# Query and key stacks of two cross attentions moved from tile to tile instead of by DRAM, and token scales spread by TensorE, in a two-layer decoder

## The chip, the cores and the metric

The kernel runs on one core of one Trainium2 chip. The metric is the time of one execution on the device in microseconds (us), the median of several runs. Lower is better. The trace is of one further execution, taken by the hardware profiler.

## What is computed

The input x is 8 batches of 256 tokens with 512 channels, a context of the same size goes with it, and everything is float32. Two decoder layers follow each other. Every block adds to x and normalises (post-norm):

```python
x = _layernorm(x + _L0_attn_ref(x, ...))            # power attention, 16 heads of 128
x = _layernorm(x + _L0_xattn_ref(x, ctx, ctx))      # 16 heads of 32, causal softmax
x = _layernorm(x + _L0_ffn_ref(x, ...))             # router, 8 bases, shared expert
x = _layernorm(x + _L1_attn_ref(x, ...))            # multi-query, plus a memory
x = _layernorm(x + _L1_xattn_ref(x, ctx, mask, ...))# 16 heads of 32, int8-like projections
x = _layernorm(x + _L1_ffn_ref(x, ...))             # 8 experts of 16, top 2
```

The change concerns the two cross attentions. The first uses x itself as queries and the context as keys and values, without projections:

```python
scores = einsum('bhqd,bhkd->bhqk', q, kj) * SCALE   # causal; then softmax, times values
```

The second quantises x by token (a scale `sx` for each token), projects it with quantised weights, and so needs each token's scale as a factor along the token axis of the projected queries:

```python
s = maximum(max(abs(x), axis=-1) / 127, EPS); qx = clip(round(x / s), -127, 127)
q = einsum('bnc,oc->bno', qx, qw) * (sx * sw) + bq
```

## The kernel before

Tokens are worked on in four groups g of two batches (512 tokens), and channels in four chunks kc of 128, which are four heads of 32. Six stages follow each other, overlapping at their ends: the first attention until about 760 us of the trace, the first cross attention until 1078, the first feed-forward until 1650, the second attention until 2045, and then the second cross attention with the last feed-forward.

**Stacks.** float32 products are made of two parts each, a high part rounded to fp32r and the rest as a low part, as high*high + low*high + high*low. In the cross attentions a head has 32 channels, so the three products fit on top of each other in one contraction of 96 rows: the queries are stacked as (high, low, high), `QO = (0, 1, 0)`, and the keys as (high, high, low), `KO = (0, 0, 1)`. A stack is a tile of 96 partitions by 4 heads by 512 tokens. The parts are made with 128 channels on 128 partitions (4 heads of 32). To become a stack, head j's 32 partitions must move to partitions 32i to 32i+31 of part i. Before, that goes by DRAM: `stack_out` (line 1101) writes the high and the low part, 256 KB each, to a buffer of the ring `rs` (four buffers), and `stack_in` (line 1107) reads three transfers of 256 KB, one for each part i, into the stack.

**First cross attention** (`l0_xattn`). For each of 16 chunks (g, kc), `stacks` turns x (TensorE), makes the high part xh on ScalarE (L1218) and the low part xl on VectorE (L1222), and sends both out. Both tiles have one buffer (`bufs=1`). `keys` sends out the context's parts cth and ctl, and `stacked` reads both stacks into `qs[kc % 2]` and `ks[kc % 2]`: tiles b_q and b_k for even chunks, two tiles named b_pair for odd ones. The first two chunks are made earlier, during the first attention, by `first_stacks`, through their own DRAM buffers bq and bk. `attend` then makes, for two batches and four heads, scores (TensorE, L1331), maxima (VectorE, L1345), exponentials (ScalarE, L1352), transposes (L1365), and sums with the values (L1381). Beside it run `later_keys` and `later_values`: keys and values of the second cross attention, kept in DRAM (ke, ve) until they are read there.

**Second cross attention** (`l1_xattn`). `Quantising` finds each token's scale on VectorE (L1549 to L1551), rounds on GpSimd, and turns the result by TensorE through the PSUM bank m2 (one buffer). `scales_out` sends the 512 scales (tile xts) to a DRAM buffer dsx (L2223, single words) and reads them back into all 128 partitions as tile sxb (L2225). `queries_keys` projects (L2243), multiplies by both scales on VectorE (tq, L2247), makes th (ScalarE, L2251) and tl (VectorE, L2255), one buffer each, and sends both out. `load` has `stacked` read the query stack back and the key stack from ke, and `values` read v (L2278). `attend` makes scores (L2291), maxima with the mask (L2306), exponentials (L2315), transposes (L2329) and sums (L2348). In the last group (g = 3) the two batches are worked on one after the other and each reads its half of the stack.

**What sets the order.** All DMAs of these stages are issued by SyncE (SP), in order: one that waits holds all behind it. The order on every engine is made before the kernel runs. Each step of the work is entered with a planned time (`plan.at`). `listed` then plays the whole program: at each point it takes, among the steps that may go within a window (`W_A` to `W_D`, `WINDOW`) and a slack (`SLACK`) of the earliest start, the one with the earliest planned time, moved by an amount for its kind from the table `MOVED`. Durations come from `occupied`, with the latencies `LP`, `LA` and `LV`. Every engine is then held to the order found. So a change of these constants can move any instruction of the program.

Of the kernel before, what the change touches and what calls it, by code (L numbers as in the profile page):

```python
# [13 lines left out]
F32 = mybir.dt.float32  # L14
# [7 lines left out]
P = 128  # L22
# [17 lines left out]
SB, W_A, W_B, W_C, WC, WDD = -3000, 26.2, 23.9, 17.8, -5, -30  # L40
LP, LA, LV = 0.325, 0.235, 0.215
SE, WINDOW, SLACK, QL_D, ML_D, W_D, QX_D, TP = -350.0, 35.5, 0.033, 20, 14, 22.8, 0, 10
# [6 lines left out]
def occupied(i, mode):  # L49
# [44 lines left out]
    ("Ctx", "load_tokens"): -4.45,  # L94
    ("Loading", "high"): 4.8,
    ("Loading", "load"): 8.85,
    ("Loading", "low"): -3.6,
    ("Norming", "apply"): 8.25,
    ("Norming", "minus"): -2,
    ("Norming", "scale"): 7.15,  # L100
    ("Norming", "stats"): 3.5,
    ("Pool", "close"): -4.25,
    ("Pool", "open"): 1.05,
    ("Prepared", "high"): 2.35,
    ("Prepared", "load"): 1.7,
    ("Prepared", "low"): 6.15,
    ("Prepared", "scale"): 2.7,
    ("Prepared", "scales"): 0.85,
    ("Prepared", "store"): 0.5,
    ("QKV", "open"): 5.05,  # L110
    ("Quantising", "out"): -8.85,
    ("Quantising", "scale"): 1.9,
    ("Quantising", "turn"): -2.95,
    ("Quantising", "whole"): -5.4,
    ("Transposing", "high"): -4.2,
    ("Transposing", "low"): -7.3,
    ("Transposing", "turn"): -11.85,
    ("l0_attn", "add"): -0.15,
    ("l0_attn", "constants"): 4.05,
    ("l0_attn", "decay"): 7.05,  # L120
    ("l0_attn", "decay_broadcast"): 4,
    ("l0_attn", "high"): 2.45,
    ("l0_attn", "load"): 2.25,
    ("l0_attn", "log_sigmoid"): 6.65,
    ("l0_attn", "low"): -4.9,
    ("l0_attn", "mul"): -12,
    ("l0_attn", "norms_turn"): -10.3,
    ("l0_attn", "out"): -2.05,
    ("l0_attn", "proj"): 5.15,
    ("l0_attn", "scores"): 2.7,  # L130
    ("l0_attn", "split"): 11.15,
    ("l0_attn", "split_gate"): -1.4,
    ("l0_attn", "square"): -4.4,
    ("l0_attn", "sums"): 4.5,
    ("l0_attn", "sums_out"): 4.4,
    ("l0_attn", "turn"): -3.55,
    ("l0_ffn", "act"): -5.65,
    ("l0_ffn", "add"): 1.4,
    ("l0_ffn", "choose"): -3.2,
    ("l0_ffn", "counts"): 2.9,  # L140
    ("l0_ffn", "down"): -0.5,
    ("l0_ffn", "load"): 3.6,
    ("l0_ffn", "logits"): -0.3,
    ("l0_ffn", "logits_out"): -8.55,
    ("l0_ffn", "mixtures"): 3.95,
    ("l0_ffn", "mul"): -12,
    ("l0_ffn", "proj"): -3.75,
    ("l0_ffn", "split"): 1.55,
    ("l0_ffn", "turn"): 0.9,
    ("l0_ffn", "turn_back"): 3.35,  # L150
    ("l0_xattn", "add"): 3.9,
    ("l0_xattn", "bias"): 0.45,
    ("l0_xattn", "constants"): -5.8,
    ("l0_xattn", "high"): -0.95,
    ("l0_xattn", "keys"): 9.4,
    ("l0_xattn", "load"): -11.6,
    ("l0_xattn", "load_bias"): -1.25,
    ("l0_xattn", "load_context"): 2.75,
    ("l0_xattn", "low"): 0.7,
    ("l0_xattn", "maxima"): -2.4,  # L160
    ("l0_xattn", "more_constants"): 2.6,
    ("l0_xattn", "out"): 1.75,
    ("l0_xattn", "probs"): 6.05,
    ("l0_xattn", "proj"): 4.8,
    ("l0_xattn", "scale"): -5.8,
    ("l0_xattn", "stacked"): -8.7,
    ("l0_xattn", "sums"): 1.9,
    ("l0_xattn", "sums_out"): 8.6,
    ("l0_xattn", "turn"): 6.25,
    ("l0_xattn", "turn_back"): 7.3,  # L170
    ("l0_xattn", "values"): 10.95,
    ("l1_attn", "add"): 4.8,
    ("l1_attn", "elu_exp"): 5.65,
    ("l1_attn", "elu_relu"): 2.65,
    ("l1_attn", "elu_split"): -2.75,
    ("l1_attn", "high"): -7.6,
    ("l1_attn", "keys_high"): 1.55,
    ("l1_attn", "keys_in"): -0.5,
    ("l1_attn", "keys_values_tiles"): -12,
    ("l1_attn", "low"): -12,  # L180
    ("l1_attn", "memories"): 2.35,
    ("l1_attn", "memory_add"): -1.4,
    ("l1_attn", "memory_out"): 5.6,
    ("l1_attn", "memory_scale"): -1.15,
    ("l1_attn", "out"): -8.75,
    ("l1_attn", "probs"): 2,
    ("l1_attn", "proj"): -1.55,
    ("l1_attn", "queries_in"): -4.7,
    ("l1_attn", "reduce"): 8.3,
    ("l1_attn", "scale"): 12,  # L190
    ("l1_attn", "scores"): 3.2,
    ("l1_attn", "split"): 8.3,
    ("l1_attn", "sums"): 12,
    ("l1_attn", "sums_out"): -7.7,
    ("l1_attn", "turn"): 4.95,
    ("l1_attn", "values_copy"): 4.15,
    ("l1_attn", "values_out"): -0.55,
    ("l1_attn", "weights"): 11,
    ("l1_ffn", "act"): -12,
    ("l1_ffn", "act_add"): 1.6,  # L200
    ("l1_ffn", "act_tanh"): -5.55,
    ("l1_ffn", "add"): -0.35,
    ("l1_ffn", "choose"): -6.45,
    ("l1_ffn", "chosen"): 3.1,
    ("l1_ffn", "gate"): -0.95,
    ("l1_ffn", "gated"): 0.6,
    ("l1_ffn", "proj"): -2.4,
    ("l1_ffn", "split_low"): 0.8,
    ("l1_ffn", "turn"): -0.9,
    ("l1_ffn", "up"): 0.5,  # L210
    ("l1_ffn", "weights"): -9.55,
    ("l1_ffn", "write"): -5.45,
    ("l1_xattn", "add"): -0.6,
    ("l1_xattn", "bias_x"): -1.4,
    ("l1_xattn", "high"): -4.7,
    ("l1_xattn", "low"): -5.85,
    ("l1_xattn", "masks_in"): 1.7,
    ("l1_xattn", "maxima"): 0.3,
    ("l1_xattn", "out"): 2.15,
    ("l1_xattn", "probs"): 0.7,  # L220
    ("l1_xattn", "proj"): -0.2,
    ("l1_xattn", "put"): -2.5,
    ("l1_xattn", "scale"): -5.3,
    ("l1_xattn", "scales_out"): 8.55,
    ("l1_xattn", "scores"): 2.2,
    ("l1_xattn", "stacked"): -1.7,
    ("l1_xattn", "sums"): 6.05,
    ("l1_xattn", "sums_out"): -7.85,
    ("l1_xattn", "sums_turned"): 8.4,
    ("l1_xattn", "turn"): 1.75,  # L230
    ("l1_xattn", "turn_back"): 3.8,
    ("l1_xattn", "values"): -6.6,
# [877 lines left out]

def halves_in(K, dst, d, order):

    for i in range(2):
        for part, s in enumerate(order):
            ins = K.nc.sync.dma_start(
                f32(dst[64 * i + 16 * part : 64 * i + 16 * part + 16]),
                d[s].rearrange("(p i d) t -> i d p t", i=2, d=16)[i],
            )
    return ins
# [34 lines left out]
def l0_xattn(K, plan, before, late_from, pair, wk, bk, wv, bv):  # L1154
# [49 lines left out]
    def stacks(plan, t0, src, kc, pool, tag, scale, ring, out):  # L1204
# [15 lines left out]
        def low():  # L1220
            l = pool.tile([P, 512], FR, tag=tag + "l", name=tag + "l", bufs=1)
            nc.vector.scalar_tensor_tensor(l, whole(), scale, f32(st["h"]), ALU.mult, ALU.subtract)  # L1222
            stack_out(K, out(), st["h"], l)
# [5 lines left out]

    def stack(u, n):  # L1230
        u[n] = K.dram.tile([2, P, 512], F32, tag="rs", name="rs", bufs=4)
        return u[n]

    def first_stacks(us):
# [11 lines left out]
        for kc in range(2):  # L1246
            us[kc]["qd"], us[kc]["kd"] = (K.scratch(f"b{n}{kc}", [2, P, 512]) for n in "qk")
            t = U_A * (20 + 2 * kc)
            stacks(before, t, lambda: c["t"], kc, pre, "k", 1.0, None, lambda kc=kc: us[kc]["kd"])
            stacks(before, t + U_A, lambda: K.x[0], kc, pre, "q", SCALE, "v", lambda kc=kc: us[kc]["qd"])  # L1250

    def queries_keys(t0, g, kc, c, u):


        def keys():
            stack_out(K, stack(u, "kd"), c["t"].h[:, kc, :], c["t"].l[:, kc, :])
# [1465 lines left out]
```

## Time and profile before

| | |
|---|---|
| median of 3 runs | 2397.88 us (2394.03 to 2402.05) |
| profiled execution, its own time | 2399.13 us |
| its span in the trace | 2397.4 us |
| granted TensorE clock, mean | 0.958 |
| TensorE, VectorE, ScalarE, GpSimd busy | 91%, 63%, 46%, 30% |
| moved by DMA | 226.83 MB, 36.0% of 16 engines' span |

Busy time in the stages (us):

| stretch | PE | DVE | ACT | DMA share |
|---|---|---|---|---|
| 0 to 760 | 731.56 | 461.16 | 325.06 | 0.20 |
| 760 to 850 | 66.54 | 59.93 | 49.00 | 0.60 |
| 850 to 1078 | 205.11 | 130.57 | 137.53 | 0.71 |
| 1078 to 1650 | 548.40 | 292.91 | 116.49 | 0.27 |
| 1650 to 2045 | 358.57 | 291.25 | 207.53 | 0.43 |
| 2045 to 2110 | 54.31 | 47.64 | 49.88 | 0.73 |
| 2110 to 2397 | 227.01 | 222.81 | 208.55 | 0.46 |

In the trace PE is TensorE's matmuls, PEld its weight loads, DVE is VectorE, ACT ScalarE, POOL GpSimd, SPq the queue of SyncE. L1107 is line 1107 of the kernel. `b_pair<-rs` is an operation that writes tile b_pair and reads rs. The chain is the work that ended last, followed back from the end. "A <- B: 13.9, 17, 3.6" says that A waited for B for 13.9 us in all, 17 times, at most 3.6.

### The profile page before, as it was taken

To read this page: it belongs to the slowest core of one execution; us is meant where nothing else is said; L and a number is where in the kernel's file an instruction comes from. 1 tells how busy PE (TensorE), PEld (TensorE's weight loads), DVE (VectorE), ACT (ScalarE), POOL (GpSimd) and SP (SyncE) were. 2 spreads that over 40 slices of the span, in tenths; PEclk is the share of its full clock that TensorE was granted. 3 is DMA by queue.
4 is the path that set the end of the run, shared out by engine and by line. 5 is a ranking of instruction groups with operands and counts; after the bars stand their busy time and mean duration, and the time that the engine had idled before them with its cause. 6 is when DMAs were issued, how large, how long until landed. Compare 5 with 4: busy or idle time off the path is not lost.

```text
span 2397.4 us, 36873 instructions
## 1 busy us (share of the span) xinstructions
PE 2191.5 (91%) x12779; PEld 1670.0 (70%) x12800; DVE 1506.3 (63%) x3563; ACT 1094.0 (46%) x2697; POOL 718.0 (30%) x978
## 2 busy tenths in 40 slices
PE   7999999899999689988989999998999997878885
PEld 5888877688887567666778778886556564546663
DVE  5655666656556655555655554444777876778885
ACT  3443444444444565654211321112456554678884
POOL 3544444544444211111112201001112323523233
PEclk9999999999999899998999999999799998899997
DMA  4111122112112777752563201103454353765630
GB/s 141 49 40 45 58 76 71 45 57 80 40 36 84 201 215 206 205 167 80 56 147 119 69 33 53 36 1 98 84 93 87 79 92 78 172 157 141 177 80 36
DMA packets 146266, 226.83 MB, mean 95 GB/s; under 512 B 23680, under 2 KB 46848, under 8 KB 145824
## 3 DMA queue, kind: packets, MB, share of 16 engines
q1 hardware_dynamic: 146080, 224.48, 36.0%
q8 instruction: 102, 1.67, 0.3%
q14 instruction: 84, 0.69, 0.1%
HBM read 162.43 MB, written 57.79 MB: 92 GB/s over the span
## 4 chain that ended last, share of the span: by engine, by line
PE 65%; DVE 14%; DMA 7%; ACT 7%; issue 4%; POOL 2%; SPq 1%; ACTq 0%; DVEq 0%; POOLq 0%
PE v L665 5%; PE v L667 5%; PE v L666 5%; PE w L667 3%; PE w L665 3%; PE w L666 3%; PE mm L652 3%; PE mm L665 3%; PE mm L667 3%; PE mm L666 3%; PE z L665 2%; PE z L667 2%; PE z L666 2%; PE w L652 2%; PE z L652 2%
## 5 line engine op out<-in xcount | busy, mean ns | idle before, releaser
L1038 POOL TENSOR_TENSOR x<-x,ot 128x512 f32<-128x512 f32 x128 | 171.7, 1341 | 261.3 <-ACT ot L1037 199.8
L2029 DVE TENSOR_REDUCE nm<-w 128x2 f32<-128x512 f32 x256 | 166.1, 684 | 44.7 <-PE w L652 44.2
L2072 ACT ACTIVATE pr<-v 128x512 f32<-128x512 f32 x256 | 139.4, 595 | 81.3 <-PE v L652 80.7
L1701 ACT ACTIVATE sg<-w 128x512 f32<-128x512 f32 x64 | 38.1, 598 | 258.1 <-PE w L667 245.7
L1037 ACT ACTIVATE ot<-m,rn 128x512 f32<-128x512 f32 x128 | 88.0, 687 | 79.6 <-PE m L667 76.7
L2329 PE MATMUL w<-ident,pr 128*128 128x128 f32 x512 | 97.1, 297 | 27.3 <-ACT pr L2315 21.2
L1352 ACT ACTIVATE pr<-w,nm 128x128 f32<-128x128 f32 (+1 forms) x256 | 105.3, 425 | 27.9 <-DVE nm L1345 12.2
L1034 DVE SCALAR_TENSOR_TENSOR x<-mm,rn,x 128x512 f32<-128x512 f32 x128 | 95.3, 745 | 31.1 <-PE mm L667 30.1
L665 PE MATMUL w<-wgh,ph 128*128 128x512 f32 x256 | 102.1, 399 | 2.7 <-ACT sg L1701 2.7
L666 PE MATMUL w<-wgl,ph 128*128 128x512 f32 x256 | 101.2, 395 | 3.4 <-DVE wgl L1591 3.4
L2329 PEld LDWEIGHTS w<-ident,pr 128*128 128x128 f32 x512 | 61.0, 146 | 59.6 <-ACT pr L2315 54.9
L1345 DVE TENSOR_REDUCE nm<-w 128x1 f32<-128x128 f32 (+1 forms) x256 | 77.4, 347 | 39.5 <-PE w L1340 29.5
L667 PE MATMUL w<-wgh,pl 128*128 128x512 f32 x256 | 101.2, 395 | 0.0
L1410 POOL TENSOR_TENSOR x<-x,oo 128x256 f32<-128x256 f32 x32 | 24.7, 773 | 240.5 <-DVE oo L1406 240.5
L1590 POOL TENSOR_SCALAR wgh<-raw 128x512 fp32r<-128x512 f32 x40 | 26.1, 654 | 226.1 <-PE w L667 182.8
L1704 DVE TENSOR_TENSOR sg<-sg,v 128x512 f32<-128x512 f32 x42 | 28.8, 686 | 97.8 <-PE v L667 87.7
L636 DVE TENSOR_TENSOR yl<-y,yh 128x512 fp32r<-128x512 f32 x64 | 44.0, 688 | 70.3 <-ACT yh L635 70.3
L635 ACT ACTIVATE yh<-y 128x512 fp32r<-128x512 f32 x64 | 38.2, 597 | 108.8 <-PE y L667 106.1
L978 DVE TENSOR_TENSOR a<-w,se 128x512 f32<-128x512 f32 (+1 forms) x128 | 67.5, 549 | 21.6 <-PE w L667 19.0
L986 ACT ACTIVATE a<-a 128x768 f32<-128x768 f32 x64 | 54.0, 844 | 55.9 <-DVE a L978 55.9
L2115 POOL TENSOR_TENSOR x<-x,oo 128x256 f32<-128x256 f32 x32 | 23.4, 730 | 185.7 <-DVE oo L2104 148.3
L994 DVE TENSOR_TENSOR al<-a,ah 128x768 fp32r<-128x768 f32 x64 | 69.2, 1083 | 13.8 <-POOL ah L990 13.5
(609 smaller groups left out, 7227.2 us busy)
## 6 DMA issues: line engine op xcount, KB each, us to landing
q<-rs SPq DMA_DIRECT2D x90, 128.0 KB, 3.5
b_pair<-rs SPq DMA_DIRECT2D x42, 256.0 KB, 5.6
q<-rs SPq DMA_DIRECT2D x36, 256.0 KB, 4.2
k<-ke SPq DMA_DIRECT2D x36, 256.0 KB, 6.1
raw<-in_Wq_dram SPq DMA_DIRECT2D x32, 256.0 KB, 2.7
eb<-lg SPq DMA_DIRECT2D x32, 256.0 KB, 3.5
raw<-in_Wc_dram SPq DMA_DIRECT2D x32, 256.0 KB, 3.4
raw<-in_L_ffn_w_gate_dram SPq DMA_DIRECT2D x32, 256.0 KB, 4.0
```

The costliest lines, as they stand in the source:

```text
L652: ins = self.K.nc.tensor.matmul(*args, **kw)
L665: nc.tensor.matmul(ps, lh, rh, start=first, stop=False)
L666: nc.tensor.matmul(ps, lh, rl, start=False, stop=False)
L667: nc.tensor.matmul(ps, ll, rh, start=False, stop=last)
L1034: nc.vector.scalar_tensor_tensor(xt, st["o", r], c, xt, ALU.mult, ALU.add)
L1037: nc.scalar.activation(ot, st["o", r], AF.Copy, scale=c)
L1038: nc.gpsimd.tensor_tensor(xt, xt, ot, ALU.add)
L1345: nc.vector.tensor_reduce(m[:, t : t + 1], st["w", j][:, t, : (t + 1) * P], AX.X, ALU.max, negate=True)
L1352: nc.scalar.activation(p_[:, t * P : (2 * t + 1) * P], st["w", j][:, t, : (t + 1) * P], AF.Exp, bias=st["m", j][:, t : t + 1], accum_out=s ...
L2029: nc.vector.tensor_reduce(st["nm"][:, :, h], st["w", h], AX.X, ALU.max, negate=True)
L2072: nc.scalar.activation(st["p", h], st["w", h], AF.Exp, scale=SCALE)
L2329: ins = nc.tensor.transpose(v[:, sb, t * P : (t + 1) * P], st["p", j][:, t, sb * P : (sb + 1) * P], K.ident)
```

## The change

Query and key stacks are no longer sent by DRAM. The new function `stack_through` fills one part i of a stack by four transfers, one for each head, straight from the high or the low tile: 32 partitions by 512 tokens, 64 KB each, twelve for a stack. In the first cross attention that is done for 14 of the 16 chunks, queries and keys (the first two stay as they were); in the second for the queries of groups 0 to 2 (the last group, and all keys, stay). So xh, xl, th, tl and the context's parts are read by these transfers themselves, and no `rs` buffer stands between. The token scales are spread by TensorE: four matmuls whose stationary operand is one column of the scales repeated 128 times and whose moving operand is the identity leave every token's scale in all partitions of bank m2, and ScalarE copies it to sxb. The planner's constants and its whole table `MOVED` have new values.

```diff
-SB, W_A, W_B, W_C, WC, WDD = -3000, 26.2, 23.9, 17.8, -5, -30
-LP, LA, LV = 0.325, 0.235, 0.215
-SE, WINDOW, SLACK, QL_D, ML_D, W_D, QX_D, TP = -350.0, 35.5, 0.033, 20, 14, 22.8, 0, 10
+SB, W_A, W_B, W_C, WC, WDD = -3000, 22.2, 24.0, 17.8, -5, -30
+LP, LA, LV = 0.320, 0.230, 0.210
+SE, WINDOW, SLACK, QL_D, ML_D, W_D, QX_D, TP = -350.0, 35.5, 0.03, 20, 14, 22.8, 0, 10
...
 MOVED = {
-    ("Ctx", "load_tokens"): -4.45,
-    ("Loading", "high"): 4.8,
+    ("Ctx", "load_tokens"): 0.85,
+    ("Loading", "load"): 4.8,
...
+def stack_through(K, dst, halves, order, i):
+
+    for j in range(4):
+        K.nc.sync.dma_start(f32(dst[32 * i : 32 * i + 32, j]), f32(halves[order[i]][32 * j : 32 * j + 32]))
...
     def queries_keys(t0, g, kc, c, u):
-        def keys():
-            stack_out(K, stack(u, "kd"), c["t"].h[:, kc, :], c["t"].l[:, kc, :])
...
+        def queries(i):
+            u["q"] = qs[kc % 2]
+            stack_through(K, u["q"], u["h"], QO, i)
+
+        def keys(i):
+            u["k"] = ks[kc % 2]
+            stack_through(K, u["k"], [v[:, kc, :] for v in (c["t"].h, c["t"].l)], KO, i)
...
         if "qd" not in u:
-            stacks(plan, t0 - 14, lambda: K.x[g], kc, one, "x", SCALE, "v", lambda: stack(u, "qd"))
-            plan.at(t0 - 13, keys)
-        (late if kc % 2 else plan).at(t0 - 8.6, stacked)
+            stacks(plan, t0 - 14, lambda: K.x[g], kc, one, "x", SCALE, "v", halves)
+            for i in range(3):
+                (late if kc % 2 else plan).at(t0 - 8.5 + 0.6 * i, queries, i)
+                (late if kc % 2 else plan).at(t0 - 8.4 + 0.6 * i, keys, i)
+        else:
+            (late if kc % 2 else plan).at(t0 - 8.6, stacked)
...
     def scales_out(c):
-        dsx = K.dram.tile([512], F32, tag="dsx", name="dsx")
-        nc.sync.dma_start(dsx.rearrange("(n p) -> p n", p=P), c["x"].s)
+        c["b"] = K.bank("m2")
+        for t in range(4):
+            nc.tensor.matmul(
+                c["b"][:, t * P : (t + 1) * P], c["x"].s[:, t : t + 1].to_broadcast([P, P]), K.ident, start=(t == 0), stop=(t == 3)
+            )
+
+    def scales_in(c):
         c["s"] = xp.tile([P, 512], F32, tag="sxb", name="sxb")
-        nc.sync.dma_start(c["s"], dsx.rearrange("(o c) -> o c", o=1).to_broadcast([P, 512]))
+        nc.scalar.activation(c["s"], c["b"], AF.Copy)
...
-            u["d"] = K.dram.tile([2, P, 512], F32, tag="rs", name="rs", bufs=4)
-            stack_out(K, u["d"], st["h"], l)
+            u["h"] = st["h"], l
+            if g == 3:
+
+                u["d"] = K.dram.tile([2, P, 512], F32, tag="rs", name="rs", bufs=4)
+                stack_out(K, u["d"], st["h"], l)
...
+        def queries(i):
+            u["q"] = qkv.q[1 - kc % 2][:96]
+            stack_through(K, u["q"], u["h"], QO, i)
...
-        plan.at(t0 - 11, stacked)
+        if g == 3:
+            plan.at(t0 - 11.5, stacked)
+        for i in range(3 if g < 3 else 0):
+            plan.at(t0 - 11.4 + 1.5 * i, queries, i)
+        plan.at(t0 - 11, keys)
         plan.at(t0 - 6, values)
...
         plan.at(tx + dx * 3 + 1.2, scales_out, c)
+        plan.at(tx + dx * 3 + 2.2, scales_in, c)
```

## The prediction

> **What bounds the kernel now.** I read the page first: busy times, then the chain that ended last.
>
> ```profile
> span 2397.4 us, 36873 instructions
> ...
> PE 2191.5 (91%) x12779; PEld 1670.0 (70%) x12800; DVE 1506.3 (63%) x3563; ACT 1094.0 (46%) x2697; POOL 718.0 (30%) x978
> ...
> PE 65%; DVE 14%; DMA 7%; ACT 7%; issue 4%; POOL 2%; SPq 1%; ACTq 0%; DVEq 0%; POOLq 0%
> ```
>
> TensorE is busy for 2191.5 of 2397.4 us, so all that can be won without taking its work away is its 206 us of idle time. DMA holds 7% of the chain, some 168 us; that is not a gain, because much of it lies beside a busy TensorE. What counts is where TensorE thins out while the chain is in a transfer. So I read the busy time in slices of ten us (columns: stretch, PE, PEld, DVE, ACT and POOL busy, TensorE clock, DMA share, GB/s), and the chain of the same stretch.
>
> ```profile
> 2020.00:2030.00 10.00, 9.46 (x87) 5.99 (x85) 8.51 (x21) 5.79 (x12) 0.73 (x1) 1.00 0.25 61
> 2030.00:2040.00 10.00, 4.66 (x25) 3.06 (x26) 3.81 (x13) 2.10 (x4) 0.19 (x1) 0.75 0.45 92
> 2080.00:2090.00 10.00, 6.74 (x49) 4.25 (x51) 6.02 (x26) 6.54 (x23) 7.93 (x8) 0.98 0.63 162
> 2110.00:2120.00 10.00, 7.86 (x57) 4.83 (x60) 7.36 (x27) 8.20 (x27) 0.00 (x0) 1.00 0.88 215
> 2120.00:2130.00 10.00, 5.51 (x30) 3.12 (x30) 3.84 (x12) 2.58 (x6) 2.61 (x4) 0.69 0.82 208
> 2130.00:2140.00 10.00, 6.27 (x43) 4.72 (x42) 8.30 (x33) 7.05 (x26) 3.88 (x5) 0.97 0.56 155
> ```
>
> ```profile
> 2069.45 12.39 DMA dsx<-xts
> 2081.86 5.40 DMA sxb<-dsx
> ...
> 2109.37 5.01 DMA rs<-th
> ...
> 2117.90 7.50 DMA rs<-tl
> 2127.73 6.74 DMA rs<-th
> ```
>
> The token scales go to DRAM as single words (dsx) and come back spread over 128 partitions (sxb): 12.39 and 5.40 us on the chain. The second transfer waits for the first at the head of SP's queue, and everything SP has to issue stands behind it, as SP's own timeline shows (start, duration, instruction):
>
> ```profile
> 2096.18 0.38 SPq L2223 DMA_DIRECT2D dsx<-xts  x1
> 2108.63 0.34 SPq L2225 DMA_DIRECT2D sxb<-dsx  x1
> 2109.37 0.34 SPq L1101 DMA_DIRECT2D rs<-th  x1
> ```
>
> For 12.4 us SP issues nothing; the stack rs<-th leaves right after. The same happens at 2020.75 to 2029.83, 2069.45 to 2081.86 and 2191.41 to 2200.07. The waits of SP from 2045 us on put 31.7 us on sxb behind dsx.
>
> The other stage touched is the first cross attention, steady from 850 to 1078 us (its row of busy times, TensorE's longest wait there, and three rows of the list of DMA issues: count, KB each, us to landing):
>
> ```profile
> 850.00:1078.00 228.00, 205.11 (x1422) 158.28 (x1414) 130.57 (x367) 137.53 (x517) 36.18 (x79) 0.99 0.71 203
> ```
>
> ```profile
> PE w L1331 <- ACT pr L1352: 13.9, 17, 3.6
> ```
>
> ```profile
> b_pair<-rs SPq DMA_DIRECT2D x42, 256.0 KB, 5.6
> ...
> rs<-th SPq DMA_DIRECT2D x32, 256.0 KB, 2.0
> ...
> q<-mx SPq DMA_DIRECT2D x44, 64.0 KB, 2.5
> ```
>
> Here the DMA engines are 71% busy, but TensorE waits for ScalarE's exponentials, not for stacks. So little is to be had there.
>
> **A. Scales: dsx and sxb go.** Eight transfers vanish. An undisturbed slice (2000 to 2030) has 9.14, 8.92 and 9.46 us of TensorE, mean 9.2. Against that the five slow slices lack 4.5, 2.5, 1.3, 3.7 and 2.9 us, together 14.9: the far end of the gain. The near end is 4.1 us, the one wait that TensorE itself shows in there (v L652 for q<-mx, at 2036, a transfer that SP issued directly behind sxb). What is late next: between 2110 and 2140 th and tl, each one buffer, are waited for until their transfers have read them (5.01, 7.50, 6.74 us). After the change eight transfers read th and four tl; at 0.40 us each on SP (row of b_pair and q<-rs: medians 0.41 and 0.43) twelve take 4.8 us to issue and 2.5 to land, 7.3 in all, about as long. So of the 6.6 us of the last two slices I count half. Taken: 4.5+2.5+1.3+3.3 = **-11.6** (-14.9 to -4.1, before the next point).
>
> The clock column shows a second loss, 0.75 in the slice from 2030 and 0.69 in that from 2120: at full clock their work would take 4.66 x 0.25 + 5.51 x 0.31 = 2.9 us less. That comes back only if the gaps close altogether, so it goes to the far end: -17.8.
>
> **B. What replaces them.** Sixteen matmuls (four a group) and four ScalarE copies. The trace has no float32 matmul of 128x128 that isn't a transpose. Bounds: 0.12 us (sums L2348: 16 in 1.87 us) and 0.79 us (up projection into w L667), so 1.9 to 12.7; taken the transposes of the same size, 0.29 (L2179), 4.6 us, of which half falls into the gaps of A: **+2.3** (0 to +16). The fourth waits for DVE's last scale at the head of TensorE's queue, in two groups with four transposes and the next scores behind it: at most DVE's three instructions for a scale (0.60 + 0.16 + 0.17 us at 2010.15), 3.7 us over four groups, which I put into the upper bound. The bank m2 is single, so the quantiser's transposes wait for the copy. Copies: 4 x 0.60 (L2182) = 2.4, at nothing, because ScalarE is busy 49.9 of 65 us from 2045 to 2110; without that cover +2.4.
>
> **C. Stacks of the first cross attention.** 28 stacks (14 chunks, queries and keys) each lose two transfers out and three in and gain twelve of 64 KB. Bytes: the 56 transfers out, 14.7 MB, go; those in stay, read from SBUF. SP: 28 x 7 = 196 more issues x 0.40 = 78 us, beside SP's waits of about 190 us between 760 and 1078 (the sum of its longest rows there), which hide it; without that cover +78. The first four transfers of a query stack wait at the head of SP's queue until the scores of two chunks before have read the tile; behind them stand the context loads and the keys and values going out. That wait is there now too (SP for PE w L1340: 18.4 us, 6 times, 6.2 the longest). New is that xh and xl, one buffer each, are held along with it, where four DRAM buffers stood between: ScalarE's next xh, and the exponentials behind it, can wait as long, 18.4 us in all. No row shows this transfer; the nearest, also from tile to tile and also 64 KB, is q<-mx, 2.5 us. Gain: chain and slices meet at two places, 830 to 840 (5.98 us of TensorE, chain in ctxT 7.08 behind six b_pair<-rs) and 890 to 900 (6.40, chain in rs<-cth 2.70); against 9.2 they lack 3.2 and 2.8. Three stacks' bytes still go in, so half: **-3.0** (-14.6 if these close in full, and 2.6 and 6.0 us from 790 to 810 too; +18.4 if xh waits as said; more only by rival 1).
>
> One rule speaks against this. The Trainium skill, "DMA: Bandwidth & Descriptors", section "Rules for kernel authors", says to merge many small transfers, since below 64 KB one pays mostly overhead. If the twelve came one after another at the row's 2.5 us, a stack would take 30 us and 28 stacks 840 us; against the issue pace of 0.40 us, 4.8 + 2.5. SP issued two q<-mx within 1.23 us at 2030.26, less than one landing, so they overlap, and I go by the issue pace.
>
> **D. Stacks of the second cross attention.** Twelve query stacks (groups 0 to 2) go the same way: 84 issues x 0.40 = 34 us on SP, beside some 170 us of waits there that remain without those on dsx and rs (234 less 31.7, 28.8 and 2.9). The chain's rs<-th at 2208.54 (8.42 us) lies in 2200 to 2240, where TensorE has 34.41 of 40 us, like its neighbours (35.53, 35.34). **-1** (-3 to +5).
>
> **E. The order.** Every planned time, window and slack is new. In the built order 8,568 of 11,890 TensorE instructions keep their place relative to each other, and the amount of work is the same except for B and two fewer ACT table loads in the first feed-forward (1.27 and 1.28 us each on the chain, at L1656 and L1738): half, **-1.3**. Beyond that a new order can give or take; bounds +-8, from the 28 us that TensorE idles before 760 and the 24 from 1078 to 1650. I take none.
>
> **Sum** against the profiled execution: its span 2397.4 plus 1.7 around it is 2399.1. 2399.1 - 11.6 + 2.3 - 3.0 - 1.0 - 1.3 = 2384.5. It lies 1.2 above the median of the three runs shown, so on their footing **2383**.
>
> **Rivals.**
> 1. *SP's pace becomes the bound of the first cross attention* (slower). In the built program a DMA waits for the one issued eight before it, so eight landings bound the pace. A chunk then holds 24 + 5 transfers; chunks last 18.95 us now (b_q loads at 851.7 and 1041.2, ten chunks apart). The rival decides from a landing of 18.95 x 8 / 29 = 5.2 us on. b_pair<-rs lands in 5.6, b_k<-rs in 6.6; midway, 6.1, a chunk takes 22.1 us, +3.2 in 13 chunks, +41: 2383 + 3 + 41 = 2427. For it: those rows write the same 32 partitions. Against: they are four times as large and come six in a row; q<-mx lands in 2.5.
> 2. *The gaps were cover* (no change). From 2140 on DVE, ACT and TensorE are all 80 to 90% busy, and the last 50 us hang on one block's chain, so a gap closed is given back. Only 2030's 4.5 stays, less B: 2396.
> 3. *All thin slices close*: A in full, C's 14.6, E's 2.6: 2397.9 - 17.8 - 14.6 - 2.6 - 1 + 2.3 = 2364.
> 4. *It doesn't do what it says*: the built order has 480 transfers from tile to tile and no dsx, so this is excluded; only the first two chunks of the first cross attention and the last group of the second still go by DRAM.
>
> **Chances.** Forecast 0.44, rival 3 0.18, rival 2 0.20, rival 1 0.12, an order or a held xh that costs some 25 us 0.06 (2383 + 25 = 2408). A measurement can tell 0.3%, 7 us. Faster 0.44 + 0.18 = 0.62; same 0.20; slower 0.12 + 0.06 = 0.18. Range: from 2356 (rival 3 and the order's 8) to 2412 (the forecast with C's +18.4 for its -3 and the order's +8), leaving out 0.06 below, in rival 3, and 0.12 above, rival 1.
>
> **What would show it.** A right: 2030 to 2040 and 2080 to 2140 (shifted) near 9 us of TensorE, no SP gap over 8 us after xts. B: sixteen matmuls of 0.2 to 0.4 us. C: through transfers landing in 2.5 to 4 us, DMA share from 0.71 to about 0.55 (14.7 MB less of the 64 that 203 GB/s move from 760 to 1078). Wrong: landings above 5.2 us, SP waiting for DMA in the first cross attention, or TensorE's wait at L1331 naming DMA; or TensorE's idle time growing in stages that the stacks don't touch.

## The result, and the profile after

| | before | after |
|---|---|---|
| median, runs of one chip | 2395.45 us (5 runs, 2390.89 to 2402.05) | 2413.64 us (5 runs, 2409.47 to 2422.16) |
| ratio, 95% interval | | 1.0067 (1.0040 to 1.0095) |
| span of the profiled execution | 2397.4 us | 2420.4 us |
| moved by DMA | 226.83 MB | 204.85 MB |

The changed kernel is slower by 18 us, where 2383 was forecast. Its profiled execution took 2422.16 us, the longest of its five runs, 8.5 above their median. An execution of 4590 us among the experiments below was disturbed and is left out of its ratio. The page of the changed kernel, busy times and chain:

```profile
span 2420.4 us, 37282 instructions
...
PE 2202.4 (91%) x12808; PEld 1679.5 (69%) x12832; DVE 1519.7 (63%) x3563; ACT 1092.6 (45%) x2699; POOL 723.0 (30%) x978
...
PE 61%; DVE 17%; ACT 7%; DMA 5%; issue 4%; SPq 3%; POOL 2%; DVEq 0%; ACTq 0%; POOLq 0%
```

DMA has gone from 7% of the chain to 5%, as meant, and SP's queue from 1% to 3%. To see where the time went, one event at the end of each stage is taken from both traces: the first and the last score of the first cross attention that gets its mask (tile dm), the last activation of the first feed-forward (ScalarE writes sg from w), the first and last use of the mask in the second cross attention (tile mn, read where the row maxima are taken), and the end.

| stretch (us) | before | after |
|---|---|---|
| start to the first masked score | 770.7 | 791.9 |
| first cross attention | 317.7 | 333.0 |
| to the last sg | 547.7 | 537.5 |
| to the second cross attention | 422.1 | 423.1 |
| second cross attention | 285.4 | 272.1 |
| to the end | 53.8 | 62.8 |

The second cross attention, where the scales are, gains 13 us. The first loses 15, and it starts 21 later. The stretch behind it gives 10 back, and the end loses 9. The two slices that were thinnest before (4.66 us of TensorE in 2030 to 2040, 5.51 in 2120 to 2130) have no match in the slices of after (same columns as in the prediction; 7.28 is the least from 2050 to 2170). One of them, at 2070, still has a low clock, 0.66:

```profile
2070.00:2080.00 10.00, 8.23 (x43) 4.39 (x43) 2.86 (x11) 3.89 (x8) 3.31 (x4) 0.66 0.56 130
2110.00:2120.00 10.00, 8.62 (x68) 5.96 (x67) 9.49 (x39) 7.92 (x28) 6.93 (x7) 1.00 0.84 194
2120.00:2130.00 10.00, 8.65 (x69) 5.96 (x68) 8.50 (x34) 8.40 (x28) 9.66 (x9) 1.00 0.66 138
2130.00:2140.00 10.00, 7.28 (x54) 5.33 (x56) 7.02 (x23) 9.30 (x29) 1.88 (x2) 1.00 0.40 98
```

The matmuls that spread the scales cost what was said: all 16 keep TensorE busy for 4.66 us, 0.29 each. The trace has two records for each, which overlap (duration in ns: least, median, most):

```profile
L2244 PE MATMUL m<-ident,xts x32: 272/275/377, 2062.6 to 2227.7; 128*128 128x128 f32 x32
```

Now the first cross attention, 850 to 1085 us. Its row before, and its row after:

```profile
850.00:1085.00 235.00, 211.98 (x1478) 163.61 (x1469) 134.62 (x379) 141.99 (x535) 36.18 (x79) 0.99 0.71 202
```

```profile
850.00:1085.00 235.00, 198.47 (x1312) 152.27 (x1312) 125.58 (x344) 132.33 (x481) 32.31 (x74) 0.93 0.51 143
```

The DMA engines' share has gone from 0.71 to 0.51 and the rate from 202 to 143 GB/s, and TensorE does 13.5 us less in the same time. So the load on the DMA engines was not what held it. SP's timeline shows what does. First a stretch of before, then one of the changed kernel (start, duration, instruction; a piece of several transfers can hold short waits):

```profile
874.64 0.42 SPq L1101 DMA_DIRECT2D rs<-cth  x1
875.12 0.44 SPq L1101 DMA_DIRECT2D rs<-ctl  x1
882.89 1.27 SPq L1107 DMA_DIRECT2D b_q<-rs  x3
884.21 1.37 SPq L1107 DMA_DIRECT2D b_k<-rs  x3
```

```profile
869.07 1.18 SPq L1120 DMA_DIRECT2D b_q<-xh  x2
870.29 2.48 SPq L1120 DMA_DIRECT2D b_q<-xl  x4
872.82 2.49 SPq L1120 DMA_DIRECT2D b_q<-xh  x4
875.35 5.02 SPq L1120 DMA_DIRECT2D b_k<-cth  x8
880.47 0.54 SPq L1335 DMA_DIRECT2D ve<-ve  x1
```

In the second, each piece begins where the one before ends: SP issues without a break. Added up transfer by transfer over 850 to 1085, SP is issuing for 71 us (30%) before and waits for 157; after, it is issuing for 195 us (83%) and waits for 36. (Shares of SP below are counted in the same way, without its waits.) One transfer takes it 0.588 us (median), about 0.63 from start to start, and they land soon (2.0 us, least 1.9, median 2.0, most 6.5 in the whole trace):

```profile
L1120 SPq DMA_DIRECT2D b_k<-cth x48: 507/589/1782, 875.4 to 1082.7; - x48
```

The same kind of row was there before, for the transfers that the prediction itself called the nearest, and it read their landing only:

```profile
L1151 SPq DMA_DIRECT2D q<-mx x44: 585/592/1662, 1690.0 to 2042.5; - x44
...
L1107 SPq DMA_DIRECT2D b_k<-rs x18: 376/430/432, 853.0 to 1042.6; - x18
```

At the stage's start the chain of after names transfers (start, duration):

```profile
779.18 12.02 DMA b_k<-bk
...
824.30 7.35 DMA raw<-in_L_xattn_wkT_dram
```

The loads of the first stacks, b_q<-bq and b_k<-bk, now leave SP at 775 to 777 us, behind the context's loads; before they left at 752.8 and 757.2. That is the new order, not the way of the stacks.

### The profile page after: what moved, and what is told of

Its sections match the earlier page's. It is cut to its first block, busy times and chain, and to the rows that moved or that the text cites. A ratio compares the mean times of both kernels' runs of the same rounds, so it can differ in the third digit from the quotient of the medians.

```text
span 2420.4 us, 37282 instructions
## 1 busy us (share of the span) xinstructions
PE 2202.4 (91%) x12808; PEld 1679.5 (69%) x12832; DVE 1519.7 (63%) x3563; ACT 1092.6 (45%) x2699; POOL 723.0 (30%) x978
## 2 busy tenths in 40 slices
DMA packets 137821, 204.85 MB, mean 85 GB/s; under 512 B 25984, under 2 KB 49152, under 8 KB 137376
## 4 chain that ended last, share of the span: by engine, by line
PE 61%; DVE 17%; ACT 7%; DMA 5%; issue 4%; SPq 3%; POOL 2%; DVEq 0%; ACTq 0%; POOLq 0%
PE v L671 5%; PE v L673 5%; PE v L672 5%; PE w L673 3%; PE w L671 3%; PE w L672 3%; PE mm L658 3%; PE mm L671 3%; SPq L1120 2%; PE z L673 2%; PE z L672 2%; PE z L671 2%; PE mm L673 2%; PE mm L672 2%; DVE nm L2048 2%
## 5 line engine op out<-in xcount | busy, mean ns | idle before, releaser
L1429 POOL TENSOR_TENSOR x<-x,oo 128x256 f32<-128x256 f32 x32 | 23.4, 732 | 203.0 <-DVE oo L1425 171.9
L1000 DVE TENSOR_TENSOR al<-a,ah 128x768 fp32r<-128x768 f32 x64 | 78.9, 1233 | 2.7 <-POOL ah L996 2.7
L996 POOL TENSOR_SCALAR ah<-a 128x768 fp32r<-128x768 f32 x64 | 55.5, 867 | 64.7 <-ACT a L992 64.5
```

The costliest lines, as they stand in the source:

```text
L1000: nc.vector.tensor_tensor(st["al", b], st["a", b], f32(st["ah", b]), ALU.subtract)
```

## The experiments

Theory 1: the loss is SP's time to issue the through transfers (0.59 us and not 0.40). Theory 2: the loss is the new order. Each run has its ratio to the kernel before on the same chip; that kernel's median there was 2401.26 us for the order and the three parts each alone; 2405.57 for scales and second together, the three parts in the old order, one planned time set back, and the keys on GpSimd's queue alone; 2390.62 for the two runs with two buffers in the first cross attention alone, the nine transfers, and the twelve reads in a block; and 2404.72 for the rest.

### The parts, each alone

**Order alone.** Code of before; planned times and constants of after.

```diff
-SB, W_A, W_B, W_C, WC, WDD = -3000, 26.2, 23.9, 17.8, -5, -30
+SB, W_A, W_B, W_C, WC, WDD = -3000, 22.2, 24.0, 17.8, -5, -30
...
-    ("l0_xattn", "stacked"): -8.7,
+    ("l0_xattn", "stacked"): -0.6,
```

> The kernel before with the new planner constants and the new table, and none of the new transfers or matmuls: the order alone. Theory 1 (SP's issue time: a transfer from tile to tile takes SP 0.585 us to issue, not 0.40, and fills SP in the first cross attention) expects the order alone within 8 us of before, ratio 0.997 to 1.003. Theory 2 (the new order is the loss: the stacks of the first chunk stand behind the context's loads at 776 us, and weights behind other transfers) expects 10 to 20 us slower, 1.004 to 1.008.

Measured: 2433.98 us, ratio 1.0139 (1.0113 to 1.0166), 33 us slower, more than either theory said. Its trace is read from a further run, below.

**Scales alone.** Code of before with `scales_out` and `scales_in` of after.

> The kernel before, with old constants, and only the token scales spread by TensorE. Both theories expect a gain, 4 to 12 us (2386 to 2392 beside 2396), because SP's three holds of 9 to 12 us on dsx go; the forecast had 9.3 less for this (11.6 less 2.3). No change would say that those gaps were cover.

Measured: 2381.13 us, ratio 0.9917 (0.9892 to 0.9943), 20 us faster, more than the 4 to 12 expected. Busy time from 2020 us on, in before and with the scales alone:

```profile
2020.00:2140.00 120.00, 92.72 (x648) 59.04 (x653) 80.65 (x285) 77.99 (x232) 41.18 (x45) 0.89 0.66 153
```

```profile
2020.00:2133.50 113.50, 98.16 (x759) 64.10 (x760) 86.90 (x308) 86.51 (x259) 44.38 (x48) 0.93 0.67 163
```

111 more matmuls are done 6.5 us earlier, and the clock granted is higher. The gain is made behind the first feed-forward, whose last sg still comes 3 us later than before (1638.9 for 1636.1): the stage from first to last mn, where dsx stood, shrinks from 285.4 to 268.6 us, and the end stays as it was (54.6 for 53.8).

**First cross attention alone**, by through transfers, as in the diff of the change.

> The kernel before, with old constants (the moved steps have their new entries), and only the stacks of the first cross attention from tile to tile. Theory 1: 10 to 25 us slower, the stage from the first masked score to the last longer by that, SP's issues of these transfers 0.58 us each and on the chain. Theory 2: within 5 us of before.

Measured: 2415.82 us, ratio 1.0065 (1.0043 to 1.0086), 14.6 us slower; the stage 336.9 us for 317.7; SP issuing 80% of 850 to 1085.

**Second cross attention alone.**

> The kernel before, with old constants, and only the query stacks of groups 0 to 2 of the second cross attention from tile to tile. Theory 1: within 5 us, since SP has some 170 us of waits there and 144 x 0.585 less 60 x 0.40 is 60 us more. Theory 2: the same, so this one tells only whether the stage gains by itself.

Measured: 2412.33 us, ratio 1.0049 (1.0029 to 1.0070), 11 us slower, where theory 1 said within 5. Between 2040 and 2200 us SP issues for 55% of the time (27% before), and it still stands behind dsx besides (27.4 us, 3 times).

**Scales and second together.**

> Scales by TensorE and the second cross attention's stacks tile to tile, the first cross attention by DRAM, in the planned times of the kernel before. Scales alone: 2381.1, second alone: 2412.3 against 2401.3. Theory 1 says the second's loss is SP solid with transfers of 0.62 us where the dsx transfers also held SP for 9 to 12 us: without dsx the loss shrinks to 0 to 5 us, 2381 to 2386, ratio 0.992 to 0.994. Rival (84 more issues of 0.6 us cost their 11 us whatever else SP does): 2392, ratio 0.996.

Measured: 2394.64 us, ratio 0.9946 (0.9928 to 0.9963), between the two expectations, with an interval that reaches both. Against the scales alone it is 0.29% slower, 7 us, where the second alone cost 0.49%. That the dsx waits made part of the loss is likely and not shown.

**All three parts in the old order.**

> All three parts of the change (scales by TensorE, the stacks of both cross attentions tile to tile) in the planned times and constants of the kernel before; the only new planned times are those of the steps that did not exist. The parts run alone gave -20.1 (scales), +14.6 (first cross attention) and +11.0 (second). Theory 1 (the loss is SP's issue time, part by part): the sum, +5.5, so 2407, ratio 1.002; less, down to 2396, if the second's loss needed the dsx waits that the scales take away. Theory 2 (the new order is a loss of its own of about 12 us): as theory 1 here, and the changed kernel at 2413.6 then stands 7 to 18 us above this run for its order. Rival (the parts hinder each other, the new order costs nothing): 2412 to 2416 here too, ratio 1.006.

Measured: 2408.65 us, ratio 1.0009 (0.9995 to 1.0024). The parts add up: -0.54% with scales and second, +0.65% with the first, gives +0.11%. So code alone makes no difference, and the changed kernel's 0.67% less 0.09% leaves 0.58% (14 us; by both intervals some 6 to 21) to the order.

### The order

**One planned time set back** in the changed kernel:

```diff
-    ("l0_xattn", "stacked"): -0.6,
+    ("l0_xattn", "stacked"): -8.7,
```

> The changed kernel with one planned time set back: the step that brings the stacks of the first two chunks of the first cross attention from DRAM at -8.7 as in the kernel before, not at -0.6. In the changed kernel these loads leave SP at 775 to 777 us (757 before), TensorE has 1.83 of 10 us in 780 to 790 and waits 7.6 us for b_k. Theory 2 (the order is part of the loss, and here): the first masked score comes 8 to 13 us earlier than 791.9 and the kernel takes 2401 to 2406 us, ratio 1.000 to 1.002. Rival (these 8 us are given back inside the stage, since SP's issue pace bounds its chunks anyway): no more than 3 us, 2411 to 2414, ratio 1.004 to 1.006.

Measured: 2413.29 us, ratio 1.0031 (1.0015 to 1.0047). The first masked score comes 11.3 us earlier (780.6), as expected. The stage is 4.4 us longer (337.4), so the last one is 6.9 earlier. Of 1.0067 about half is left; the time lies between the two expectations. That it is SP's pace that takes part of it back is likely and not shown.

**Order alone, for its trace** (one execution).

> The code of the kernel before with the planned times and constants of the changed one (the run that took 2434, ratio 1.0139), for its trace. Theory 2 (where the order loses): the stacks of the first two chunks are loaded at about 776 us behind the context loads, so the first masked score comes 15 to 22 us later than 770.7, and the rest of the 33 us lies behind the first cross attention's last score. Rival: the start of the first cross attention comes within 8 us of before, and the loss is inside the stages.

Measured: 2434.68 us. The first masked score comes at 783.6, 12.9 us later than before, between what was expected; the stage takes 330.0 for 317.7 without a single through transfer; the second cross attention 300.7 for 285.4, and the end 59.7 for 53.8; 9 and 2 us come back in between. TensorE's waits from 775 to 1115 us, and one from 2050 to 2380:

```profile
PE w L1337 <- ACT pr L1358: 29.4, 41, 2.1
PE mm L671 <- ACT ekh L733: 12.6, 1, 12.6
PE w L1337 <- DMA b_k<-bk: 5.3, 1, 5.3
```

```profile
PE v L2297 <- DMA k<-ke: 13.4, 1, 13.4
```

Before, the first of these is 15.4 us and the ekh wait 4.4; no wait of the last kind is among the longest. All but the first name a load that leaves SP later than before: b_k<-bk at 771.68 us for 757.18, the last wkT (which ekh needs) at 815.83 for 806.92, and k<-ke. The last one stands behind a scales transfer in SP's queue:

```profile
2114.69 0.92 SPq L2229 DMA_DIRECT2D dsx<-xts  x1
2129.26 0.34 SPq L2231 DMA_DIRECT2D sxb<-dsx  x1
...
2132.37 2.35 SPq L1113 DMA_DIRECT2D k<-ke  x3
```

From 2115 to 2129 SP issues nothing, and k<-ke follows. The changed kernel has no dsx, so this wait behind it can't be part of what the order costs there; that may be why the order costs 33 us on the old code and some 14 in the changed kernel. So the order loses at three places here, and what each planned time did there was not taken apart, beyond the one above.

### What in the first cross attention loses

The following change only that stage, from the run with it alone (336.9 us, 1.0065); the last two start from the kernel before.

**Key transfers on GpSimd's queue**:

```diff
-        K.nc.sync.dma_start(f32(dst[32 * i : 32 * i + 32, j]), ...)
+        (K.nc.sync if order is QO else K.nc.gpsimd).dma_start(f32(dst[32 * i : 32 * i + 32, j]), ...)
```

> The first cross attention alone tile to tile (as the run that took 2415.8, 336.9 us from first to last masked score against 317.7 before), but the twelve transfers of each key stack are issued by GpSimd's queue, which has 36 of 228 us busy in this stage, and those of the query stack by SP. The bytes, the tiles, the landings' size and the planned times stay. Theory 1 (SP's issue time, 24 x 0.62 = 15 us of a chunk's 19): SP has 7.5 us a chunk again, the stage falls to 318 to 324 us and the kernel to 2401 to 2406, ratio 1.000 to 1.002. Rival 1 (the traffic itself, many transfers of 64 KB writing 32 partitions, or the held xh): the stage stays at 334 to 337, the kernel at 2414 to 2417, ratio 1.006. Rival 2: GpSimd's issue of a transfer takes over 1 us each, then keys come late and the stage is as long or longer with TensorE or SP waiting for GpSimd.

Measured: ratio 1.0034 (1.0022 to 1.0045), stage 326.5 us, SP issuing 47%. About half of the loss is gone, between theory 1 and rival 1. GpSimd takes 0.51 us for each (mean; 168 in all), so rival 2 falls. What is left can be read from ScalarE's waits, 850 to 1085:

```profile
ACT xh L1225 <- DMA b_pair<-xh: 9.4, 5, 3.2
...
ACT xh L1225 <- DMA b_q<-xh: 6.8, 3, 3.6
```

ScalarE can't write the next xh until the transfers that read the last one have landed: 16.2 us. That is the price that the prediction put at 18.4 at most.

**The same, and two buffers for xh and xl**:

```diff
-            st["h"] = pool.tile([P, 512], FR, tag=tag + "h", name=tag + "h", bufs=1)
+            st["h"] = pool.tile([P, 512], FR, tag=tag + "h", name=tag + "h", bufs=2 if tag == "x" else 1)
...
```

> As the run with the key stacks' transfers on GpSimd's queue (first cross attention 326.5 us, against 336.9 with all on SP and 317.7 before), and the halves xh and xl of the query stack get two buffers each. In that run ScalarE's next xh still waited 16.2 us between 850 and 1085 for the through transfers that read the last one, and VectorE's xl 14.9 us behind it. Theory 1b (what is left of the loss is the held xh): the stage falls to 317 to 321 us, the kernel to a ratio of 1.000 to 1.002. Rival (what is left is the later arrival of the stacks, or GpSimd's 168 issues of 0.51 us): the stage stays at 325 to 327, ratio 1.003.

Measured: 2381.74 us, ratio 0.9963 (0.9948 to 0.9979), 8.9 us faster than before; stage 308.2 us. That is better than theory 1b said. So the way by DRAM cost something, a good part of it at the stage's start: from 770 to 860 us TensorE is busy 71.81 us here and 66.28 before. The two buffers alone don't explain it: before, ScalarE's xh waits for no transfer in this stage, so they would free nothing there (no run by DRAM has them). SP and ScalarE's xh are both out of the way:

```profile
850.00:1085.00 235.00, 208.44 (x1454) 159.30 (x1452) 137.29 (x381) 140.08 (x523) 106.93 (x222) 1.00 0.53 153
```

**The two buffers alone**, all transfers on SP.

> The first cross attention alone tile to tile, all on SP (336.9 us for the stage, ratio 1.0065), with two buffers for xh and xl and nothing else. Theory 1 (SP's issue time comes first, 15 of a chunk's 19 us, and the held xh only behind it): the stage stays above 331 us, ratio 1.005 or more. Rival (the held xh is the whole loss, and half the transfers on another queue only let it go sooner): 318 to 324, ratio 1.000 to 1.002.

Measured: ratio 1.0074 (1.0053 to 1.0094), stage 331.7, SP 81%. Buffers without a free queue bring nothing that the ratio shows. Theory 1 holds: SP comes first, the held xh behind it.

**Nine transfers for twelve**, all on SP, xh with one buffer:

```diff
+    i = (i, (0, 2, 1)[i])[order is KO]
+    if i and order[i] == 0:
+        K.nc.sync.dma_start(f32(dst[32 * i : 32 * i + 32]), f32(dst[:32]))
+        return
     for j in range(4):
```

> The first cross attention alone tile to tile, all on SP, but the third of each stack that repeats the high halves is copied by one transfer of 256 KB from the part of the stack that has just arrived, so nine transfers a stack for twelve. Theory 1: 18 x 0.62 = 11.2 us a chunk for 15, SP has 3.7 us a chunk again, and xh is let go after the first eight; the stage falls from 337 to 324 to 330 us, ratio 1.002 to 1.005. Rival (bytes or landings, not issues): the bytes are the same and the last transfer waits for the first four to land, so the stage stays at 337 or grows, ratio 1.0065 or more.

Measured: ratio 1.0004 (0.9989 to 1.0020), stage 315.4, SP 68%: the bytes are the same, and the loss is gone. It is better than expected, and the rival (bytes, landings) falls. The high tile is also let go after eight of the nine, so this run relieves both SP and xh.

**By DRAM, but twelve reads of 64 KB a stack**, where before had three of 256 KB:

```diff
+    for i, s in enumerate(order):
+        for j in range(4):
+            K.nc.sync.dma_start(f32(dst[32 * i : 32 * i + 32, j]), d[s, 32 * j : 32 * j + 32])
...
-                stack_in(K, u[n], u[n + "d"], order)
+                (stack_in if kc < 2 and g == 0 else stack_in_parts)(K, u[n], u[n + "d"], order)
```

> The kernel before, by DRAM as it was, but each stack of the first cross attention comes from DRAM in twelve transfers of 64 KB where there were three of 256 KB (the first two chunks keep three). Same bytes as before, the same number of transfers into the stacks as in the change, another kind of issue: reads from DRAM took SP 0.42 us, transfers from tile to tile 0.585. Theory 1 (issue time, not the count of transfers): 24 x 0.45 + 4 x 0.36 = 12.2 us a chunk and about 2 for the rest, below its 19, and xh isn't held; the stage is 318 to 326 us, ratio 1.000 to 1.003. Rival (the count and the size of 64 KB are the loss): the stage goes to 335 or above, ratio 1.006.

Measured: ratio 1.0085 (1.0065 to 1.0105), stage 342.5: theory 1's number failed. The issue is 0.42 us as said, but SP's timeline shows the reads of a chunk's two stacks in one block, which with one transfer of 1.39 us and waits of some 2 us inside takes longer than 24 x 0.46 = 11:

```profile
957.43 13.84 SPq L1115 DMA_DIRECT2D b_pair<-rs  x24
971.36 0.37 SPq L1101 DMA_DIRECT2D ke<-uh  x1
```

Everything else stands behind it for 13.84 us, the raw loads for ScalarE's cth among it (its wait for them is 16.3 us, 8.0 before).

**The same reads planned in pieces of four**:

```diff
-        (late if kc % 2 else plan).at(t0 - 8.6, stacked)
+        if kc < 2 and g == 0:
+            (late if kc % 2 else plan).at(t0 - 8.6, stacked)
+        for i in range(0 if kc < 2 and g == 0 else 3):
+            (late if kc % 2 else plan).at(t0 - 8.5 + 0.6 * i, queries, i)
+            (late if kc % 2 else plan).at(t0 - 8.4 + 0.6 * i, into_keys, i)
```

> As the run by DRAM in twelve reads of 64 KB a stack (342.5 us for the stage, ratio 1.0085, SP occupied 84% of it), but the twelve are planned as three steps of four for the queries and three for the keys, 0.6 apart, as the change plans its transfers, where that run had one step that put 24 into SP's queue in one block of 11 to 14 us. Theory 1c (a block in the queue is the loss there: the next keys, values and context stand behind it): 318 to 326 us, ratio 1.000 to 1.003. Rival (SP's time for so many transfers is the loss wherever they stand, whatever their source): 335 to 345, ratio 1.006 to 1.009.

Measured: ratio 0.9993 (0.9978 to 1.0008), stage 320.9 in the profiled execution (2411.22 us, 7.9 above the median). Theory 1c holds: 64 KB a transfer and their number cost nothing that the ratio shows as long as SP has room (73% issuing) and the blocks are shorter (between 850 and 1085 us 11 of the 12 rows of reads had 22 or 24 and took 12 to 16 us; here the longest takes 11.4 and most less than 8). The issue share alone doesn't decide, then: 70% in blocks lost 25 us in the stage, 73% in pieces 3, and 80 to 83% in pieces 14 to 19.

### Together

**The changed kernel relieved**: its keys' transfers by GpSimd in the first cross attention, two buffers for xh and xl.

> The changed kernel itself with two edits: the key stacks' twelve transfers of the first cross attention leave by GpSimd's queue, and xh and xl of the query stack have two buffers. In the order of before the same two edits took the stage from 336.9 to 308.2 us and the ratio from 1.0065 to 0.9963. Theory 1 (the changed kernel loses in this stage, by SP's queue and the held xh): its stage falls from 333 to 305 to 313 us, the ratio from 1.0067 to 0.996 to 0.999. Rival (its new order is the loss and gives the relief back): 1.003 or more.

Measured: 2396.02 us, ratio 0.9960 (0.9938 to 0.9982), stage 310.3, although it still starts at 790.8. Theory 1 holds in the changed kernel as well.

**A version better than both**: scales by TensorE, the relieved first cross attention, the second by DRAM, in the old order.

> Scales by TensorE together with the first cross attention tile to tile, its key transfers on GpSimd's queue and two buffers for xh and xl; the second cross attention by DRAM, planned times of the kernel before. Apart they gave ratios of 0.9917 and 0.9963. If they add up: 0.988, 28 us under the kernel before. Rival (what one stage gains the next gives back, or the scales' matmuls collide): 0.991 to 0.993, no better than the scales alone.

Measured: 2381.04 us, ratio 0.9892 (0.9872 to 0.9912), 24 us under the kernel before by the medians and 26 by the ratio. The gains add up nearly in full (0.988).

## Why the prediction was wrong, point by point

**A and B, the scales: right, and too small.** Net -9.3 was said, -20 measured (-14 to -26 by the interval). Two items had been held back: half of the last two slices (3.3 us) and the clock (2.9). With both the gain would be 11.6 + 3.3 + 2.9 - 2.3 = 15.5, within that interval; how much of each came in was not taken apart, and a slice at a clock of 0.66 is still there in the changed kernel. The matmuls took 4.66 us for the 4.6 assumed, the copy to sxb 0.598 (median) for 0.60, and TensorE's waits before these matmuls add up to 2.4 us. Rival 2, that the gaps were cover, was wrong here.

**C, the first cross attention: the step that failed.** The step was "196 more issues x 0.40 = 78 us", which SP's waits of about 190 us were to hide, with -3.0 taken; alone it cost +14.6. The price was taken from the reads from DRAM (0.41 and 0.43), while the row called nearest in the next sentences, q<-mx, was read for its landing and not for its issue, 0.592; the 1.23 us for two of them, which the prediction quotes, holds that price. In issue time alone 28 stacks take 28 x 12 x 0.589 = 198 us; by DRAM they took some 28 x (2 x 0.38 + 3 x 0.41) = 56. So SP got 142 us more to do, not 78. From start to start (0.63) the 24 of a chunk hold SP for 15 us of its 19. The waits did take most of it, 157 us before and 36 after in 850 to 1085, but the stage paid before they were used up: SP's work comes in the order of the queue, and what stands behind a row of transfers comes late. The runs that gave SP room took the loss back: nearly all of it with nine transfers, half of it with half of them on another queue. The term "+18.4 if xh waits as said" was a true one: 16.2 us, seen once SP was relieved. The two are not independent, so that undoing one alone gave half (326.5) or next to nothing (331.7), and both gave more than the loss (308.2). The gain that was hoped for is real, 9 us with both undone, and was hidden under them.

**D, the second cross attention.** -1 was said (-3 to +5); alone +11, beside the scales +7. The price of an issue was mis-sized in the same way: 144 transfers x 0.59 = 85 us stand where 60 took about 24, so 61 us more, not 34. SP's share of 2040 to 2200 goes from 29% with the scales alone to 61% with both. That this is the cause here is argued, not shown: SP still waits for two fifths of that stretch, and no run relieved this stage as the first was.

**E, the order.** -1.3 was said with bounds of 8; it cost 14 in the changed kernel (6 to 21) and 33 on the old code. The bounds came from TensorE's idle time in other stages. They should have come from what the moved loads feed: b_q<-bq and b_k<-bk stand behind the context loads, and wkT leaves later. The end is the order's as well: with the order alone it takes 59.7 us, in the changed kernel 62.8, before 53.8.

**The rivals.** Rival 1 named the right place and sign, 2427 against 2413.6, and by the wrong mechanism: it was to decide from a landing of 5.2 us on, and landings were 2.0. SP's issue took its place, so that it came near was in part luck. Its own count, 24 + 5 transfers in a chunk of 18.95 us, held the answer: at 0.63 us the 24 alone take 15. The last item of the chances, an order or a held xh (2408), names two of the causes and lacks the first. Of the signs that were named, the landings of 2.5 to 4 us (2.0), the DMA share of 0.55 (0.51) and the matmuls of 0.2 to 0.4 us (0.29) all came in as for "right" or better, while SP hardly waits for DMA (1.2 us in 850 to 1085) and TensorE's wait at the scores still names ScalarE (27.7 us for 13.9). Only TensorE's idle time spoke, at the stage's start and in it. No sign asked how long SP is issuing.

**The rule of the Trainium skill** ("DMA: Bandwidth & Descriptors", "Rules for kernel authors"), to merge many small transfers, pointed the right way. Runs here show where it bites: nine transfers for twelve took the loss away, and twelve reads from DRAM in pieces cost nothing that the ratio shows. In the first cross attention the small transfers cost the issuing queue's time, not their landing.

## What to carry to other kernels

Where one transfer becomes many, read the issue time of the same kind of transfer (source and target both) on the queue that will issue it, multiply, and set it against the period of the loop: what stands behind in that queue is late before the queue is full. When a DRAM buffer goes, its buffering goes too, so ask who next writes the tile that is now read directly. A part that gains and a part that loses can stand in one diff: time each alone before judging the whole.

## What the runs showed of the hardware

- SP's time to issue a transfer depends on its kind: 0.32 to 0.44 us from a tile to DRAM, 0.38 to 0.43 from DRAM to 32 partitions (256 KB; 0.42 for 64 KB), 0.59 from tile to tile (medians of rows). GpSimd's queue took 0.51 us (mean) for the last kind.
- In long rows of transfers an issue now and then takes 1.1 to 2.1 us (2.05 the longest of the through transfers in the changed kernel). What it waits for no run here shows.
- A transfer of 64 KB from tile to tile landed after 2.0 us (median; 6.5 at most) though SP was issuing 83% of the time in the first cross attention. The transfers of single words, dsx, landed after 12.4 us in the one case where the landing is recorded, and held SP for 9 to 12 us each in the kernel before.
